# Moving rooms in SBUF so that loaded and moving operands stand at other distances modulo 512 bytes, and alternating halves in the gather

## The chip, the cores and the metric

The kernel runs on one core of a Trainium2 chip. The metric is device time in microseconds for one execution, the median of several. TensorE is called PE here, VectorE DVE, ScalarE ACT, GpSimd POOL and SyncE SP, as the profile calls them.

## The reference

There are 64 batches of 256 rows with 512 columns, and an adjacency matrix of 256 by 256 of zeros and ones. Two layers follow each other, each on a normalized and rectified copy of its input and added to that input:

```python
h = jnp.maximum(_layernorm(x, axis=-1), 0.0)
q = jnp.einsum('bnd,ed->bne', h, Wq);  k = jnp.einsum('bnd,ed->bne', h, Wk);  v = jnp.einsum('bnd,ed->bne', h, Wv)
rel = adjacency.T[None, :, :] * jnp.einsum('bnd,bmd->bnm', q, k)
rel = rel / jnp.linalg.norm(rel, axis=2, keepdims=True)
x = x + jnp.einsum('bnm,bmd->bnd', rel, v)

h = jnp.maximum(_layernorm(x, axis=-1), 0.0)
y = jnp.einsum('nm,bmd->bnd', adj, h)
x = x + jnp.einsum('bnd,do->bno', y, weight) + bias
```

## The kernel before

The batches are worked in 32 pairs, so the rows of a pair make 512. Wq and Wk are multiplied into one matrix m beforehand, so that the scores are h m h'.

A product of two float32 matrices is made of three rounds. Each operand is split into three parts: u, the value scaled and rounded to the format that PE reads in one pass; l, the rest; and s, a scaled combination of the two. The names end in those letters: h_u, h_l and hs (the third part of h, in two rooms hs0 and hs1), m_u, m_l, m_s, wv_u and so on, gy_u, gy_l, gy_s, rel_u, rel_l and rel_s. Rounds u by u and l by l are written into a PSUM bank. ACT then rescales the bank in place (L324), and round s by s is added. ACT and DVE split what comes out of a bank again (L225, L226, L228 for a part that later moves; L234, L235, L236 for one that is later loaded).

In each matrix product one operand is loaded into PE (128 by 128, the rows "PEld" of the profile) and the other moves through it. The load for the next product runs beside the current one. For one pair i the stages, each in units of one PSUM bank, are these:

- g: loaded m, moving h, 512 columns. Four units. The result goes into gy.
- v: loaded h, moving wv, 512 columns. Four units, of which two come before the scores and two after the gather. The result goes into v_low and late (one list of twelve rows; the first four are v_low).
- scores: loaded gy, moving h, 256 columns, two batches into one bank each.
- gather of pair i-1: loaded late or v_low (the second layer's h, in two parts), moving adjt (the turned adjacency), 256 columns, four units, each of two halves of a bank. The result goes into gy again.
- mix of pair i-1: loaded gy, moving w, 512 columns, four units.
- attend: loaded rel, moving late or v_low, 512 columns, four units. Then the second layer's normalization and rectification (L266, into rel_s_raw) and its split (L500, L501) follow, and POOL adds the bias (L504).

A pair has 168 products of 512 columns and 80 of 256. Between the scores and attend, the masked scores (L399) are squared and summed by ACT (L403), moved by sixteen small DMAs of SP (L439), and turned by DVE (L445). The next pair's h is likewise placed by DMAs (L280), turned by DVE (L288) into the rooms of hs, and split (L303, L305, L295). The order on each engine is fixed by a planner: each operation has an estimated cost and a due time worked out back from PE's ideal sequence, and the list is written out once and kept. The rescale of one unit is followed by the next unit's first two rounds and only then by the unit's own third round.

SBUF rooms are taken one after the other in the order in which the code first names their tags. Each takes its bytes per partition, rounded up to 32. The first room, fresh, starts at byte 16,512, which is 128 modulo 512. Rooms of whole multiples of 512 bytes keep the residue. The small rooms (ones, low_max, low_any, the statistics, the norms) move it to 32 for all that comes after them.

Of the kernel before, what the change touches and what calls it, by code (L numbers as in the profile page):

```python
# [10 lines left out]
F32R = mybir.dt.float32r  # L11
# [102 lines left out]
def kernel(  # L114
# [12 lines left out]
    P = 128  # L127
    B, N, D = x.shape
    DC = D // P
    NC = N // P  # L130
    NB = 2
    TC = NB * NC
    T = NB * N
# [9 lines left out]
    def room(name, *shape, dtype=F32, tag=None):  # L143
        return pool.tile([P, *shape], dtype, name=name, tag=tag or name)

    def parts_room(name, *shape, tag=None):
        return [room(f"{name}_{k}", *shape, dtype=F32R, tag=f"{tag or name}_{k}") for k in "uls"]
# [1 line left out]
    bank = [ps_m.tile([P, 512], F32, name=f"bank{n}") for n in range(8)]  # L149
    fresh = room("fresh", TC, D)  # L150
    ring = [room(f"x_ring{n}", TC, D) for n in range(2)]
    m_p, wv_p, w_p = (parts_room(w, DC, D) for w in ("m", "wv", "w"))
    h = [room(f"h_{k}", DC, T, dtype=F32R) for k in "ul"]
    ht, h_s = [None, None], [None, None]

    def hp(k, d):
        return h[k][:, d] if k < 2 else h_s[d // 2][:, d % 2]
    wq_sb, wk_sb = room("wq_sb", DC, D, tag="gy_u"), room("wk_sb", DC, D, tag="gy_l")
    adj_low = room("adj_low", 2, D, tag="rel_u")
    v_low = room("v_low", 4, D, dtype=F32R)  # L160
    blocks = room("blocks", TC, DC, P)
# [10 lines left out]
    def changing(tag, kind, *shape, dtype=F32):  # L172

        if rooms.get(tag, (None, None))[0] != kind:
            rooms[tag] = kind, room(f"{tag}_{kind}", *shape, dtype=dtype, tag=tag)
        return rooms[tag][1]

    def late(r):

        return v_low[:, r] if r < 4 else changing("late", "parts", 8, D, dtype=F32R)[:, r - 4]  # L180
# [16 lines left out]
        for j in range(2)  # L197
    ]
    norms = [room(f"rn{n}", NB, NC) for n in range(2)]

    V, A, G, SP = nc.vector, nc.scalar, nc.gpsimd, nc.sync
    count = {"bank": 0}
# [11 lines left out]
    def mm(out, left, right, first):  # L214
        nc.tensor.matmul(out, left, right, start=first, stop=True, skip_group_check=True)  # L215
# [15 lines left out]
    def split_left_ps(plan, ps, key, parts, names, at):  # L231
        u, l, s = (p(at) for p in parts)
        ku, kl, ks = names
        plan.add("ACT", 0.49, lambda: A.activation(u, ps, AF.Copy, scale=NEAR), [key], ku)  # L234
        plan.add("DVE", 0.6, lambda: V.tensor_sub(l, ps, f(u)), [key, *ku], kl)  # L235
        plan.add("DVE", 0.6, lambda: V.scalar_tensor_tensor(  # L236
            s, f(l), CROSS + 1.0, ps, op0=ALU.mult, op1=ALU.subtract), [key, *kl], ks)
# [3 lines left out]
    def load(plan, i, src=None, name="fresh"):  # L241

        dst = fresh if name == "fresh" else ring[i % 2]
        plan.add("SP", 0.65, lambda: SP.dma_start(out=dst, in_=xs[i]), [], keys(name, TC), lands=5.5)
# [70 lines left out]
    def unit(plan, first, second, drain):  # L315

        ps, key = next_bank()
        for cost, fn, reads in first(ps):
            plan.add("PE", cost, fn, reads, [key])
        finish(plan)  # L320
        if second is None:
            drain(ps, key)
            return
        plan.add("ACT", 0.49, lambda: A.activation(ps, ps, AF.Copy, scale=ONE), [], [key])  # L324

        def rest():
            for cost, fn, reads in second(ps):
                plan.add("PE", cost, fn, reads, [key])
            drain(ps, key)
        waiting.append(rest)  # L330
# [176 lines left out]
    def gather(plan, i, exact):  # L507
        right = adjt[0]
        for b in range(NB):
            for d0 in range(0, DC, 2):  # L510
                def first(ps, b=b, d0=d0):
                    def go():
                        for d in range(2):
                            for m in range(NC):
                                c = b * NC + m
                                lefts = [late(3 + 2 * c + k) for k in range(2)] if exact else [
                                    changing("late", "h2", 8, D)[:, c]]
                                for n, left in enumerate(lefts):
                                    mm(ps[:, ts(d, N)], left[:, ts(d0 + d, P)], right[:, m, :],
                                       d == 0 and m == 0 and n == 0)  # L520
                    needs = ["adjt", *(
                        ("late", r) for m in range(NC) for c in [b * NC + m]
                        for r in ((3 + 2 * c, 4 + 2 * c) if exact else (4 + c,)))]
                    yield 8 * HALF if exact else 8 * 0.216, go, needs

                def drain(ps, key, b=b, d0=d0):
                    split_left_ps(
                        plan, ps.rearrange("p (d n) -> p d n", d=2), key,
                        [lambda at, q=q: q[:, d0 : d0 + 2, ts(b, N)] for q in gy],
                        [[(f"gy_{k}", d0, b), (f"gy_{k}", d0 + 1, b)] for k in "uls"], None)  # L530
                unit(plan, first, None, drain)
# [52 lines left out]
    def before_pairs():  # L584
        A.activation(norms[1][:, 0, 0:1], ones, AF.Sqrt)
        for _ in range(8):
            mm(bank[7][:, :P], warm, warm, True)
        V.tensor_single_scalar(low, adj_low[:, 0].bitcast(I32), 0xFFF, op=ALU.bitwise_and)
        V.tensor_reduce(low_max, low, axis=mybir.AxisListType.X, op=ALU.max)
        m_products(0)  # L590
        mm(bank[7][0:1, 0:1], low_max, ones, True)
        V.tensor_copy(low_any, bank[7][0:1, 0:1])
        for m in range(NC):
            for n in range(NC):
                nc.tensor.transpose(bank[6][:, ts(m * NC + n, P)], adj_sb[:, n, ts(m, P)], ident)
        for e in range(1, DC - 1):
            m_products(e)
        plan = Plan()
        h_rows(plan, 0, ring[0], "x0")
        plan.run()  # L600

    with tc.manual_schedule(engines=in_order):
        before_pairs()
    gy = parts_room("gy", DC, T)
    rel_p = [room(f"rel_{k}", NB, NC, NC, P, dtype=F32R) for k in "ul"]
    adjt = []
    inexact = nc.values_load(low_any[0:1, 0:1], min_val=0, max_val=P * 0xFFF)
# [21 lines left out]
    def last_m(plan):  # L629
        for i in range(DC):  # L630
            plan.add("PE", 0.86, lambda i=i: m_products(DC - 1, (i,)), [], [("bank", i)])
            split_right_ps(plan, bank[i], ("bank", i), [lambda at, q=q: q[:, at, :] for q in m_p],
                           [[("m_u", i)], [("m_l", i)], [("m_s", i)]], i)
# [32 lines left out]
    def pairs(exact):  # L666
        count["bank"] = 4
        waiting.clear()
        rooms.clear()
        plan = Plan()  # L670
        adjt[:] = [room("adjt_r", NC, N, dtype=F32R, tag="adjt") if exact else room("adjt", NC, N)]
        plan.add("ACT", 0.49, lambda: A.copy(adjt[0].rearrange("p m n -> p (m n)"), bank[6]), [("bank", 6)], ["adjt"])
        first_turn(plan)
        last_m(plan)
        count["bank"] = 4
        turn_wv(plan)
        h_rows(plan, 1)
        h_place(plan, 25.0)
        load(plan, 2)
        first_g(plan)  # L680
        v_stage(plan, 0, exact, (0, 1))
        scores(plan, 0)
        v_stage(plan, 0, exact, (2, 3))
        turn_scores(plan, 0, by_pe=True)
        finish(plan)
        h_turn(plan)
        h_parts(plan)
        split_w(plan)
        attend(plan, 0, exact)
        for i in range(1, NP):  # L690
            last = i + 1 == NP
            load(plan, i, name=f"x{i % 2}")
            if not last:
                h_rows(plan, i + 1)
                h_place(plan)
            if i + 2 < NP:
                load(plan, i + 2)
            g_stage(plan, i)
            v_stage(plan, i, exact, (0,))
            v_stage(plan, i, exact, (1,), hold=True)  # L700
            scores(plan, i)
            gather(plan, i - 1, exact)
            while held:
                held.pop(0)()
            if last or i == 1:
                turn_scores(plan, i, by_pe=True)
            v_stage(plan, i, exact, (2, 3))
            if not last:
                if i > 1:
                    turn_scores(plan, i)  # L710
                waiting.append(lambda: (h_turn(plan), h_parts(plan)))
                mix(plan, i - 1)
            attend(plan, i, exact)
            if last:
                mix(plan, i - 1)
                gather(plan, i, exact)
            store(plan, i - 1)
        mix(plan, NP - 1)
        finish(plan)
        with tc.manual_schedule(engines=in_order):  # L720
            plan.run()
# [33 lines left out]
```

## Time and profile before

| | us |
|---|---|
| median of 3 runs | 1604.11 (1603.72 to 1604.55) |
| the profiled execution's own time | 1605.16 |
| its span | 1603.3 |
| rescale L324 on ACT, 572 times | 332.4 busy, 581 ns each |
| bias addition L504 on POOL, 128 times | 191.7 busy, 1517 ns each |
| gather, adjt by late_parts, 896 products | 124.6 busy, 282 ns each |
| mix, w_s by gy_s, 512 products | 139.9 busy, 395 ns each |
| gy_l, L228 on DVE, 128 times | 113.9 busy, 892 ns each |

The times of products are longer than the distance between two of them, because a product's record reaches from its issue to its end, and the next one is issued before that. The share of busy time of PE therefore says little about its pace; the starts of successive rows do. The page's row of the granted clock is at full speed in each of its 40 slices. A DMA of 64 KB that places h lands 2.1 us after its issue, and one of 32 KB that places the scores 1.9 us.

### The profile page before, as it was taken

How to read it: one execution, taken by the hardware profiler on the slowest of the kernel's cores; microseconds unless marked ns; L12 is line 12 of the kernel's file. 1: busy time of each engine (PE TensorE's matmuls, PEld its weight loads, DVE VectorE, ACT ScalarE, POOL GpSimd, SP SyncE). 2: the span in 40 equal slices, each digit the busy share in tenths (PEclk: the TensorE clock that was granted, in tenths of full speed). 3: DMA queues.
4: the chain of work that ended last, by engine and by line, in shares of the span. 5: the costliest groups of instructions: out<-in, count | busy, mean ns of one | idle time of the engine just before them, and what ended most of it. 6: DMA issues, size and time to landing. Idle time of an engine off the chain costs nothing.

```text
span 1603.3 us, 22542 instructions
## 1 busy us (share of the span) xinstructions
PE 1586.2 (99%) x8046; PEld 1332.9 (83%) x8046; DVE 1426.4 (89%) x2419; ACT 955.0 (60%) x1812; POOL 216.5 (14%) x167
## 2 busy tenths in 40 slices
PE   8999999999999999999999999999999999999998
PEld 5788888888888888888888888888888888888886
DVE  6998899998998988998988999889989889989886
ACT  5556566566556565665565665656565656656553
POOL 0011111011111011110111110111100111101111
PEclk9999999999999999999999999999999999999999
DMA  5431444324444224443234442244432344432311
GB/s 192 111 79 41 115 109 118 67 73 111 111 113 101 74 78 117 108 116 70 75 106 114 110 119 63 76 113 110 115 95 72 84 117 108 118 68 77 80 53 55
DMA packets 433130, 153.64 MB, mean 96 GB/s; under 512 B 389872, under 2 KB 390128, under 8 KB 433008
## 3 DMA queue, kind: packets, MB, share of 16 engines
q1 hardware_dynamic: 422784, 116.46, 30.8%
q0 software_dynamic: 8432, 32.51, 5.5%
q10 hardware_dynamic: 1792, 3.15, 0.5%
q8 instruction: 65, 1.06, 0.3%
q14 instruction: 57, 0.47, 0.1%
HBM read 70.78 MB, written 33.55 MB: 65 GB/s over the span
## 4 chain that ended last, share of the span: by engine, by line
PE 71%; DVE 16%; SPq 4%; ACT 3%; DMA 3%; issue 1%; DVEq 0%; ACTq 0%
PE bank L215 71%; SPq L439 3%; DVE st L252 3%; DVE late_parts L501 2%; DVE gy_l L228 2%; DVE gy_s L226 2%; DVE x_ring L480 1%; SPq L280 1%; DVE hs L295 1%; DVE mv L253 1%; DMA x_ring<-in_L_gnn_weight_dram 1%; DMA fresh<-in_x_dram 1%; DMA h_rel<-h_rel 1%; ACT rel_s_raw L266 1%; ACT h_rel L266 1%
## 5 line engine op out<-in xcount | busy, mean ns | idle before, releaser
L324 ACT ACTIVATE bank<-bank 128x512 f32<-128x512 f32 x572 | 332.4, 581 | 414.7 <-PE bank L215 414.0
L504 POOL TENSOR_TENSOR x_ring<-x_ring,bias_bc 128x512 f32<-128x512 f32 x128 | 191.7, 1517 | 387.4 <-ACT rel_s_raw L266 387.4
L551 POOL DMA_DIRECT2D out_dram<-x_ring x31 | 24.0, 774 | 982.1 <-DVE x_ring L542 982.1
L215 PE MATMUL bank<-w_s,gy_s 128*128 128x512 f32 x512 | 139.9, 395 | 0.2 <-ACT bank L324 0.2
L215 PE MATMUL bank<-wv_s,hs 128*128 128x512 f32 x512 | 139.9, 395 | 0.0
L215 PE MATMUL bank<-w_u,gy_u 128*128 128x512 f32 x512 | 139.6, 394 | 0.0
L215 PE MATMUL bank<-wv_u,h_u 128*128 128x512 f32 x512 | 139.4, 394 | 0.0
L215 PE MATMUL bank<-h_u,m_u 128*128 128x512 f32 x512 | 138.9, 393 | 0.3 <-DVE m_s L226 0.3
L215 PE MATMUL bank<-hs,m_s 128*128 128x512 f32 x512 | 139.1, 394 | 0.0
L215 PE MATMUL bank<-w_l,gy_l 128*128 128x512 f32 x512 | 138.6, 392 | 0.0
L215 PE MATMUL bank<-wv_l,h_l 128*128 128x512 f32 x512 | 138.0, 391 | 0.0
L215 PE MATMUL bank<-h_l,m_l 128*128 128x512 f32 x512 | 137.5, 391 | 0.1
L226 DVE SCALAR_TENSOR_TENSOR gy_s<-gy_u,bank 128x512 fp32r<-128x512 f32 x128 | 86.3, 676 | 44.1 <-ACT gy_u L225 41.9
L215 PE MATMUL bank<-adjt_r,late_parts 128*128 128x256 f32 x896 | 124.6, 282 | 0.0
L228 DVE SCALAR_TENSOR_TENSOR gy_l<-gy_s,gy_u 128x512 fp32r<-128x512 f32 x128 | 113.9, 892 | 4.3
L215 PEld LDWEIGHTS bank<-adjt_r,late_parts 128*128 128x128 f32 x896 | 115.5, 190 | 0.1
L215 PEld LDWEIGHTS bank<-w_s,gy_s 128*128 128x128 f32 x512 | 95.9, 188 | 23.5 <-ACT bank L324 0.9
L215 PEld LDWEIGHTS bank<-h_u,m_u 128*128 128x128 f32 x512 | 96.0, 188 | 23.0 <-ACT wv_u L225 0.5
L215 PEld LDWEIGHTS bank<-w_u,gy_u 128*128 128x128 f32 x512 | 96.0, 188 | 22.7
L215 PEld LDWEIGHTS bank<-h_l,m_l 128*128 128x128 f32 x512 | 96.1, 188 | 21.9 <-DVE h_l L305 0.5
L215 PEld LDWEIGHTS bank<-w_l,gy_l 128*128 128x128 f32 x512 | 96.1, 188 | 21.8
L215 PEld LDWEIGHTS bank<-hs,m_s 128*128 128x128 f32 x512 | 96.3, 188 | 21.4
(109 smaller groups left out, 3241.7 us busy)
## 6 DMA issues: line engine op xcount, KB each, us to landing
fresh<-in_x_dram SPq DMA_DIRECT2D x31, 1024.0 KB, 6.0
blocks<-h_rel SPq DMA_DIRECT2D x496, 64.0 KB, 2.1
x_ring<-in_x_dram SPq DMA_DIRECT2D x31, 1024.0 KB, 7.9
out_dram<-x_ring POOLq DMA_DIRECT2D x31, 1024.0 KB, 5.2
h_rel<-h_rel SPq DMA_DIRECT2D x464, 32.0 KB, 1.9
blocks<-in_L_gnn_Wv_dram ACTq DMA_DIRECT2D x1, 1024.0 KB, 11.2
x_ring<-in_L_gnn_weight_dram SPq DMA_DIRECT2D x1, 1024.0 KB, 12.6
out_dram<-x_ring SPq DMA_DIRECT2D x4, 256.0 KB, 2.3
```

The source lines that it names most:

```text
L215: nc.tensor.matmul(out, left, right, start=first, stop=True, skip_group_check=True)
L226: plan.add("DVE", 0.63, lambda: V.scalar_tensor_tensor(s(), f(u()), ONE, ps, op0=ALU.mult, op1=ALU.subtract), [*key, *ku], ks)
L228: plan.add("DVE", 0.6, lambda: V.scalar_tensor_tensor(l(), f(s()), -CROSS, f(u()), op0=ALU.mult, op1=ALU.add), [*ku, *ks], kl)
L252: V.bn_stats(st[:, c, :], src[:, c, :])
L253: V.bn_aggr(mv[:, c, :], st[:, c, :])
L266: A.activation(dst, src[:, c, :], AF.Relu, bias=nb[:, c : c + 1], scale=rs[:, c : c + 1])
L280: plan.add("SP", 0.65, lambda j=j, k=k: SP.dma_start(out=blocks[ts(j, S), :, :, ts(k, S)], in_=hv[ts(k, S), :, :, ts(j, S)]), keys("h_rel" ...
L324: plan.add("ACT", 0.49, lambda: A.activation(ps, ps, AF.Copy, scale=ONE), [], [key])
L439: plan.add("SP", 0.65, lambda j=j, k=k: SP.dma_start(out=pv[ts(j, S), :, ts(k, S)], in_=rv[ts(k, S), :, ts(j, S)]), [("h_rel", 0), ("h_rel ...
L501: plan.add("DVE", 0.6, lambda c=c, u=u, l=l: V.tensor_sub(late(l), raw()[:, c % 2], f(late(u))), [*k, ("late", u)], [("late", l)])
L504: plan.add("POOL", 1.4, lambda c=c: G.tensor_tensor(ring[slot][:, c, :], ring[slot][:, c, :], bias_bc, ALU.add), [], [(f"x{slot}", c)])
L551: plan.add("POOL", 0.8, lambda: G.dma_start(out=outs[i], in_=ring[slot]), keys(f"x{slot}", TC), [], lands=6.0)
```

## The change

It does three things. First, it changes the order in which rooms are first named, and adds two rooms that nothing writes or reads: "behind" of 160 bytes per partition, and "level" of 448. The three parts of w, wq_sb and wk_sb (whose rooms gy_u and gy_l take over later) and gy_s now come behind the small rooms. Second, the turned adjacency gets a room larger by 512 bytes, and lies 448 bytes into it. Third, the gather's innermost loop now runs over the two halves of the bank; before, each half was finished ahead of the other.

```diff
-    m_p, wv_p, w_p = (parts_room(w, DC, D) for w in ("m", "wv", "w"))
+    m_p, wv_p = (parts_room(w, DC, D) for w in ("m", "wv"))
-    wq_sb, wk_sb = room("wq_sb", DC, D, tag="gy_u"), room("wk_sb", DC, D, tag="gy_l")
...
     norms = [room(f"rn{n}", NB, NC) for n in range(2)]
+    room("behind", 40)
+    w_p = parts_room("w", DC, D)
+    wq_sb, wk_sb = room("wq_sb", DC, D, tag="gy_u"), room("wk_sb", DC, D, tag="gy_l")
+    gy_s = room("gy_s", DC, T, dtype=F32R)
+    room("level", 112)
...
-                        for d in range(2):
-                            for m in range(NC):
-                                c = b * NC + m
-                                lefts = [late(3 + 2 * c + k) for k in range(2)] if exact else [
-                                    changing("late", "h2", 8, D)[:, c]]
-                                for n, left in enumerate(lefts):
+                        for m in range(NC):
+                            c = b * NC + m
+                            lefts = [late(3 + 2 * c + k) for k in range(2)] if exact else [
+                                changing("late", "h2", 8, D)[:, c]]
+                            for n, left in enumerate(lefts):
+                                for d in range(2):
                                     mm(ps[:, ts(d, N)], left[:, ts(d0 + d, P)], right[:, m, :],
                                        d == 0 and m == 0 and n == 0)
...
-    gy = parts_room("gy", DC, T)
+    gy = [*(room(f"gy_{k}", DC, T, dtype=F32R) for k in "ul"), gy_s]
...
-        adjt[:] = [room("adjt_r", NC, N, dtype=F32R, tag="adjt") if exact else room("adjt", NC, N)]
+        turned_adj = room("adjt_r", NC * N + P, dtype=F32R, tag="adjt") if exact else room("adjt", NC * N + P)
+        adjt[:] = [turned_adj[:, P - 16 : P - 16 + NC * N].rearrange("p (c n) -> p c n", c=NC)]
```

The residues modulo 512 bytes, worked out from the sizes of the rooms (slices of an operand move by multiples of 512, so a room has one residue):

| room | before | after |
|---|---|---|
| m, wv (all parts), h_u, h_l, rel_u, v_low | 128 | 128 |
| w (all parts), gy_u, gy_l | 128 | 192 |
| gy_s | 32 | 192 |
| rel_l, hs, late, rel_s | 32 | 128 |
| adjt | 32 | 64 |

The text calls "distance" the residue of the moving operand less that of the loaded one. For 512-column products it was 0 in rounds u and l of g, v and mix, and 96 or -96 in round s; in attend it was 0 or 96 or -96, by the pair of rooms. For 256-column ones it was 0 in the scores and, in the gather, 0 for late and -96 for v_low. Afterwards it is 0 for every 512-column product and -64 for every 256-column one.

## The prediction, made before the changed kernel was built or run

> **What bounds the kernel now.** I read the page first. By its shares one engine is the bound:
>
> ```profile
> PE 1586.2 (99%) x8046; PEld 1332.9 (83%) x8046; DVE 1426.4 (89%) x2419; ACT 955.0 (60%) x1812; POOL 216.5 (14%) x167
> ```
>
> The clock row is full speed throughout, so pace is a matter of the products. Products overlap, so I take the pace from the timeline of PE: the difference of the starts of two rows, over the count.
>
> ```profile
> 27.22 3.89 PE L215 MATMUL bank<-h_u,m_u 128*128 128x512 f32 x16 [0.31 <-DVE m_s L226]
> 30.95 3.79 PE L215 MATMUL bank<-h_l,m_l 128*128 128x512 f32 x16
> 34.57 0.63 PE L215 MATMUL bank<-hs,m_s 128*128 128x512 f32 x2
> ...
> 755.04 1.09 PE L215 MATMUL bank<-hs,m_s 128*128 128x512 f32 x4
> 755.97 1.09 PE L215 MATMUL bank<-h_u,m_u 128*128 128x512 f32 x4
> 756.89 1.07 PE L215 MATMUL bank<-h_l,m_l 128*128 128x512 f32 x4
> 757.80 1.09 PE L215 MATMUL bank<-hs,m_s 128*128 128x512 f32 x4
> ```
>
> Sixteen h_l by m_l products in a row run at (34.57-30.95)/16 = 226 ns. Both operands lie at residue 128 (the table of residues is in the section on the change): distance 0. In the steady state, hs by m_s, at distance 96, takes 0.93/4 = 232 ns; h_u by m_u, at distance 0 but just behind such a group, takes 0.92/4 = 230; h_l by m_l behind that takes 227.5. So I read: distance 0 settles at 226.7, distance 96 costs about 6 ns a product, and some eight products behind a change of distance still pay part of it. Now the 256-column ones, in the gather, where v_low lies at distance 96 from adjt and late_parts at 0:
>
> ```profile
> 726.28 0.28 PE L215 MATMUL bank<-adjt_r,v_low 128*128 128x256 f32 x1
> 726.39 0.52 PE L215 MATMUL bank<-adjt_r,late_parts 128*128 128x256 f32 x3
> 726.75 0.27 PE L215 MATMUL bank<-adjt_r,v_low 128*128 128x256 f32 x1
> 726.87 2.43 PE L215 MATMUL bank<-adjt_r,late_parts 128*128 128x256 f32 x19
> 729.14 1.09 PE L215 MATMUL bank<-wv_u,h_u 128*128 128x512 f32 x4
> ```
>
> Nineteen at distance 0 take 2.27/19 = 119.5 ns. The four from 726.28 take 117.5, and the second v_low product 110 to 120. Distance helps here, where it hurts the 512-column ones.
>
> Is PE's pace what sets the end, though? The waits (who waited for whom: us in all, times, longest) and the timeline of DVE:
>
> ```profile
> DVE ht L288 <- PE bank L215: 8.1, 29, 0.3
> ...
> PEld bank L215 <- DVE gy_l L228: 7.2, 30, 0.7
> ```
>
> ```profile
> 736.27 1.30 DVE L288 STREAM_TRANSPOSE ht<-blocks 128x512 f32<-128x512 f32 x2 [0.28 <-PE bank L215]
> ...
> 758.39 0.16 DVE L262 SCALAR_TENSOR_TENSOR nb<-mv,rs 128x4 f32<-128x4 f32 x1
> ```
>
> Once in each pair of batches DVE waits for PE (the transposes of h may not overwrite the third part before PE's last use of it), and once PE waits for DVE (the last gy_l). Between 736.27 and nb, which ends at 758.55, the timeline shows DVE without an idle bracket: 22 us back to back. ScalarE's first rectification (L266) starts at 758.65; its other condition, the rescale L324 ahead of it, ends at 758.58, so the two paths meet within 0.03 us. From there the chain of waits goes on:
>
> ```profile
> 758.65 0.82 ACT rel_s_raw L266
> ...
> 761.40 2.31 DVE late_parts L501 x2
> ...
> 772.98 0.18 DVE rs L256
> ```
>
> It holds no PE work up to the root L258, behind which the rescale L324 stands in ScalarE's queue, for which PE's hs by gy_s waits at 773.9 (as at 725.23 a pair earlier). So a pair of 48.7 us is 11.1 us of PE, from 725.23 to 736.3, and then 37.6 us of DVE and ScalarE. Only what PE gains in the first piece comes out at the end; a gain in the other piece becomes a longer wait on gy_l or on L324.
>
> **What the Trainium skill says.** No page bears on the distance of two operands modulo 512 bytes; the trace alone prices it. "TensorE: Matmul & The Clock Gate", section Back-to-back issue gap, gives N/2.4 + 2.5 ns for a product alone: 215.8 and 109.2 ns; the trace shows 226 to 232 and 119.5, so 10 to 16 ns go elsewhere. The section LDWEIGHTS there gives columns/1.2, 107 ns for 128: as long as a 256-column product streams, half a 512-column one; so in the former load and stream share the whole time, and the two kinds need not want the same distance. "SBUF — State Buffer", section Who interferes with whom, says that PE never waits on anyone and that a DVE instruction with two SBUF inputs is held up by a GpSimd one that reads SBUF. The second agrees: gy_l takes 693 ns in the median and up to 1546, beside POOL's bias additions. That lengthens the DVE piece, and the change leaves it alone.
>
> **The change part by part.**
>
> The rooms: from their sizes, all 512-column pairs come to distance 0 (hs with m_s and wv_s, w_s with gy_s, late with rel_u, v_low with rel_l and rel_s are the ones that were not) and all 256-column pairs to -64. No instruction is added; the reserved rooms are written by none, and the queues of SP and POOL keep their order.
>
> 512 columns, in the 11.1 us piece: 32 products (two v blocks, the third parts, the first half of a mix unit). Their time now: starts from 729.14 to 736.54, 7.40 us, 231.3 ns each. Ends for the price after: 226.7 (settled) and 231.3 (no gain). The first eight follow 256-column work and mix lies at 192 where v lies at 128, so some unsettling stays: I take 229. Gain 32 x 2.3 = 74 ns.
>
> 256 columns, same piece: 8 scores products and 24 of the gather. The trace shows 96, not 64. Ends: 110 ns, the shortest gap shown, and 128: 8 ns over now, somewhat above what distance costs a 512-column product, since load and stream overlap all along. I take 114, between the 110 and the 117.5 of the mixed groups. Gain 32 x (119.5-114) = 176 ns.
>
> Halves alternating in the gather: same products, same costs, another order within one unit. The scores already alternate between halves and run at the same 120 ns, so zero by itself; up to 2 ns either way on 24 products if it matters at the new pace, inside the ends above.
>
> The tie at L266: the other condition (PE's path) ends sooner, at best 0.03 us a pair.
>
> Sum a pair: 0.074 + 0.176 + 0.03 = 0.28 us, 29 pairs of this form: 8.1 us. The other 48 256-column and 136 512-column products of a pair gain some 0.6 us and give it back as waits: cover enough that they cost nothing even if slower by a few ns. Can the 0.28 pass? DVE's idle time just ahead of the transposes is 0.28 us, and what stands before it (late_parts, waiting 0.56 us for ScalarE and PE) moves up too. The score transposes need their DMAs; between the last landing and DVE's start I find about 1 us in most pairs and 0.1 to 0.3 in some eight: these may give back a little.
>
> At the end (last pair: no next batch to place, DVE idle for 1 to 2.8 us at a time) PE is the bound: some 144 512-column products at 2.3 and 64 256-column ones at 5.5 ns: 0.33 + 0.35 = 0.7 us. The start is bound by loads and the first splits: nothing.
>
> In all 8.8 us off. The profiled span was 1603.3 us and its execution 1605.16; the median of the runs 1604.11, so I set the sum against that: 1595.3 us.
>
> **The rivals.**
>
> PE's gain passes whole, if the 37.6 us are not as rigid as I read them (PE and DVE meet there within 0.03 us, so DVE's chain might move with PE's). 5,376 x 2.3 + 2,560 x 5.5 ns = 12.4 + 14.1 = 26.5 us: 1577.6. For it: PE at 99%; against: the two waits in every pair.
>
> Only the 512-column products gain, 64 being no better than 0 for the short ones: 29 x (0.074 + 0.03) + 0.3 = 3.3 us: 1600.8. For it: scores at distance 0 behind an offset group run at 117 to 119 as well, so the 117.5 may be the disturbance and not the distance.
>
> The distance of 64 hurts the short products: at 128 ns each, the 11.1 us piece takes 32 x 8.5 = 272 ns more, 74 less for the long ones: 0.2 x 29 = 5.7 us, and a little at the end: 1610. It decides above 121.8 ns (119.5 + 74/32). For it: distance 96 hurts the long ones; against: the v_low products.
>
> The layout does not come out as computed (an unwritten room gets no space): then weights, gy and late stay at 32 and nothing changes: 1604.
>
> **How the numbers follow.** Mine 0.58, full gain 0.14, little 0.15, slower 0.10, layout 0.03. With the price of a short product from 110 to 118, mine spans 1590 to 1600. The range reaches down half way into the full gain, and up over "little" to the edge of the slower case: 1580 to 1604. 0.2% is 3.2 us, what a measurement of this kernel tells from no change. Faster: mine, full gain and a bit under half of "little": 0.79. Same: the rest of "little", the layout case, some of the slower one: 0.12. Slower: 0.09.
>
> **What would show it.** Right: s groups at 227 to 229; scores and gather under 118; PE's waits on gy_l and L324 longer by some 0.4 us a pair; the DVE piece still 37.6 us; the pair 48.4. Wrong: a period shorter by 0.8 us with those waits as before (full gain), short products at 120 (little) or above 122 (slower).

## The result, and the profile after

| | median us | runs |
|---|---|---|
| before | 1604.16 (1603.72 to 1607.27) | 5 |
| after | 1595.87 (1594.7 to 1597.74) | 5 |

The ratio is 0.9946, with a 95% interval of 0.9931 to 0.996: 8.3 us less. The forecast was 1595.3. The profiled execution has a span of 1594.1 us. All line numbers of the kernel after are seven higher: L215 is now L222, L228 is L235, L324 is L331.

The page's share line, and its chain that ended last:

```profile
PE 1566.8 (98%) x8046; PEld 1327.2 (83%) x8046; DVE 1423.1 (89%) x2419; ACT 953.1 (60%) x1812; POOL 216.2 (14%) x167
...
DVE 43%; PE 42%; ACT 5%; SPq 4%; DMA 3%; issue 2%; DVEq 0%; ACTq 0%
```

The shares hardly differ from before, and the chain does. This was the chain before, and ACT before at the rectification L266, where PE's path (through the rescale L324) meets that of DVE (through nb, which ends at 758.55 us):

```profile
PE 71%; DVE 16%; SPq 4%; ACT 3%; DMA 3%; issue 1%; DVEq 0%; ACTq 0%
```

```profile
758.00 0.58 ACT L324 ACTIVATE bank<-bank 128x512 f32<-128x512 f32 x1 [1.00 <-PE bank L215]
758.65 0.82 ACT L266 ACTIVATE rel_s_raw<-x_ring,nb,rs 128x512 f32<-128x512 f32 x1
```

Before, the two paths ended within 0.04 us of each other in 24 of 30 pairs, and the chain could follow either. Now DVE's ends later in every pair, by 0.1 us or more.

The timeline of PE after, at the gather and then where hs by m_s stood out before:

```profile
720.84 1.21 PE L222 MATMUL bank<-hs,gy_s 128*128 128x256 f32 x8
721.89 0.40 PE L222 MATMUL bank<-adjt_r,v_low 128*128 128x256 f32 x2
722.13 2.66 PE L222 MATMUL bank<-adjt_r,late_parts 128*128 128x256 f32 x22
724.63 1.08 PE L222 MATMUL bank<-wv_u,h_u 128*128 128x512 f32 x4
...
731.96 1.09 PE L222 MATMUL bank<-w_u,gy_u 128*128 128x512 f32 x4
...
752.91 1.07 PE L222 MATMUL bank<-hs,m_s 128*128 128x512 f32 x4
753.82 1.07 PE L222 MATMUL bank<-h_u,m_u 128*128 128x512 f32 x4
754.72 1.07 PE L222 MATMUL bank<-h_l,m_l 128*128 128x512 f32 x4
755.63 1.07 PE L222 MATMUL bank<-hs,m_s 128*128 128x512 f32 x4
```

Read the starts. The gather's 22 take (724.63-722.13)/22 = 113.6 ns in this pair, one of the faster ones, and the 32 long products behind them (731.96-724.63)/32 = 229.1 ns. All three rounds of h by m now go at (755.63-752.91)/12 = 226.7 ns, where one of them took 232 and unsettled its neighbours. Over the whole trace, taking all gaps of starts without a stall (under 300 ns for 512 columns, under 170 for 256), the means are:

| gap of starts, ns | before | after | all distances 0 (a run below) |
|---|---|---|---|
| 512 columns, 5,376 products | 231.2 | 227.7 | 227.0 |
| 256 columns, 2,560 products | 119.2 | 116.7 | 119.6 |

So PE alone has gained 5376 x 3.5 + 2560 x 2.5 ns = 25 us, and 8.3 arrive. Most of the rest stands in the waits (us in all, times, longest):

```profile
PEld bank L222 <- DVE gy_l L235: 18.5, 30, 1.1
...
PE bank L222 <- DVE gy_l L235: 12.5, 30, 0.9
...
PEld bank L222 <- ACT bank L331: 7.8, 23, 1.6
...
DVE ht L295 <- PE bank L222: 7.9, 29, 0.3
```

The first and the fourth were 7.2 and 8.1 us before, as the prediction shows; these are the other two before:

```profile
PE bank L215 <- DVE gy_l L228: 1.6, 5, 0.5
...
PEld bank L215 <- ACT bank L324: 3.9, 7, 1.6
```

(The two rows on gy_l are the same wait seen by the load and by the product, so they are not added.) The median stall of a pair for gy_l has grown from 0.23 to 0.56 us, that for the rescale from 0.09 to 0.23.

The table follows one pair through the two pieces of the prediction: medians over 25 pairs in the middle of the trace, in us.

| | before | after |
|---|---|---|
| first piece, PE's product after the rescale to DVE's transposes | 11.04 | 10.95 |
| of it: 8 of the scores | 1.047 | 1.033 |
| of it: 24 of the gather | 2.862 | 2.828 |
| of it: 512-column products until the transposes | 7.137 | 7.093 |
| second piece, from the transposes to PE's next such product | 37.66 | 37.41 |
| of it: transposes to the end of rs | 20.49 | 20.46 |
| of it: end of rs to the start of gy_s | 0.095 | -0.092 |
| of it: start of gy_s to the end of nb | 1.70 | 1.69 |
| of it: end of nb to the rectification | 0.095 | 0.096 |
| of it: rectification to PE's product | 15.27 | 15.25 |
| pair | 48.70 | 48.36 |

The second piece was to be rigid, and it is shorter by 0.25 us. Three quarters of that are in one row, between rs and gy_s. This is the timeline of DVE before at that spot, and then that of ACT before, in one pair:

```profile
707.89 0.17 DVE L256 TENSOR_SCALAR rs<-mv 128x4 f32<-128x4 f32 x1
708.16 0.69 DVE L226 SCALAR_TENSOR_TENSOR gy_s<-gy_u,bank 128x512 fp32r<-128x512 f32 x1
```

```profile
707.53 0.60 ACT L225 ACTIVATE gy_u<-bank 128x512 fp32r<-128x512 f32 x1 [0.41 <-PE bank L215]
```

And after, DVE and then ACT:

```profile
752.51 0.17 DVE L263 TENSOR_SCALAR rs<-mv 128x4 f32<-128x4 f32 x1
752.59 0.68 DVE L233 SCALAR_TENSOR_TENSOR gy_s<-gy_u,bank 128x512 fp32r<-128x512 f32 x1
753.30 0.69 DVE L235 SCALAR_TENSOR_TENSOR gy_l<-gy_s,gy_u 128x512 fp32r<-128x512 f32 x1
753.91 0.17 DVE L268 RECIPROCAL rs<-rs 128x4 f32<-128x4 f32 x1
754.11 0.16 DVE L269 SCALAR_TENSOR_TENSOR nb<-mv,rs 128x4 f32<-128x4 f32 x1
```

```profile
753.11 0.58 ACT L331 ACTIVATE bank<-bank 128x512 f32<-128x512 f32 x1 [0.19 <-PE bank L222]
754.37 0.81 ACT L273 ACTIVATE rel_s_raw<-x_ring,nb,rs 128x512 f32<-128x512 f32 x1 [0.68 <-DVE nb L269]
```

Before, gy_s starts at 708.16, 0.10 us after rs has ended (708.06) and 0.03 after the end of ACT's gy_u (708.13); and the bracket of gy_u shows that it waits for PE's bank. So a thread from PE ran through the middle of the DVE piece. The gap is too short for the timeline to put a bracket on it. Afterwards the record of gy_s begins before that of rs has ended, and gy_u has been ready for 0.16 us in the median. The kernel before confirms the reading by itself: in five of its pairs gy_u was ready 0.14 us or more ahead, and there, too, gy_s begins 0.09 us before rs has ended.

### The profile page after: what moved, and what is told of

Its sections match the earlier page's. It is cut to its first block, busy times and chain, and to the rows that moved or that the text cites. A ratio compares the mean times of both kernels' runs of the same rounds, so it can differ in the third digit from the quotient of the medians.

```text
span 1594.1 us, 22542 instructions
## 1 busy us (share of the span) xinstructions
PE 1566.8 (98%) x8046; PEld 1327.2 (83%) x8046; DVE 1423.1 (89%) x2419; ACT 953.1 (60%) x1812; POOL 216.2 (14%) x167
## 4 chain that ended last, share of the span: by engine, by line
DVE 43%; PE 42%; ACT 5%; SPq 4%; DMA 3%; issue 2%; DVEq 0%; ACTq 0%
PE bank L222 42%; DVE st L259 7%; DVE gy_l L235 7%; DVE x_ring L487 5%; DVE late_parts L508 5%; DVE gy_s L233 5%; DVE hs L302 4%; SPq L446 3%; DVE x_ring L549 2%; DVE mv L260 2%; ACT rel_s_raw L273 2%; SPq L287 1%; ACT gy_u L232 1%; DVE h_l L312 1%; DMA fresh<-in_x_dram 1%
## 5 line engine op out<-in xcount | busy, mean ns | idle before, releaser
L331 ACT ACTIVATE bank<-bank 128x512 f32<-128x512 f32 x572 | 332.3, 581 | 395.7 <-PE bank L222 393.3
L511 POOL TENSOR_TENSOR x_ring<-x_ring,bias_bc 128x512 f32<-128x512 f32 x128 | 191.4, 1515 | 382.3 <-ACT rel_s_raw L273 382.3
L222 PE MATMUL bank<-wv_s,hs 128*128 128x512 f32 x512 | 138.5, 392 | 0.4 <-ACT bank L331 0.4
L222 PE MATMUL bank<-w_u,gy_u 128*128 128x512 f32 x512 | 138.0, 391 | 0.0
L222 PE MATMUL bank<-wv_u,h_u 128*128 128x512 f32 x512 | 137.7, 391 | 0.0
L222 PE MATMUL bank<-w_s,gy_s 128*128 128x512 f32 x512 | 137.4, 390 | 0.4 <-ACT bank L331 0.4
L222 PE MATMUL bank<-w_l,gy_l 128*128 128x512 f32 x512 | 137.4, 390 | 0.0
L222 PE MATMUL bank<-wv_l,h_l 128*128 128x512 f32 x512 | 137.3, 390 | 0.0
L222 PE MATMUL bank<-h_u,m_u 128*128 128x512 f32 x512 | 136.5, 389 | 0.3 <-DVE m_s L233 0.3
L222 PE MATMUL bank<-h_l,m_l 128*128 128x512 f32 x512 | 136.6, 389 | 0.1
L222 PE MATMUL bank<-hs,m_s 128*128 128x512 f32 x512 | 136.3, 389 | 0.0
L235 DVE SCALAR_TENSOR_TENSOR gy_l<-gy_s,gy_u 128x512 fp32r<-128x512 f32 x128 | 113.7, 890 | 4.3
L273 ACT ACTIVATE rel_s_raw<-x_ring,nb,rs 128x512 f32<-128x512 f32 x128 | 100.6, 810 | 24.9 <-DVE late_parts L508 15.6
L222 PE MATMUL bank<-adjt_r,late_parts 128*128 128x256 f32 x896 | 115.1, 280 | 0.0
L222 PEld LDWEIGHTS bank<-w_s,gy_s 128*128 128x128 f32 x512 | 95.9, 188 | 21.1 <-ACT bank L331 1.1
L222 PEld LDWEIGHTS bank<-w_u,gy_u 128*128 128x128 f32 x512 | 96.0, 188 | 20.8
L222 PEld LDWEIGHTS bank<-w_l,gy_l 128*128 128x128 f32 x512 | 96.1, 188 | 20.7
L222 PEld LDWEIGHTS bank<-wv_l,h_l 128*128 128x128 f32 x512 | 96.1, 188 | 20.5
L222 PEld LDWEIGHTS bank<-h_u,m_u 128*128 128x128 f32 x512 | 96.0, 188 | 20.5 <-ACT wv_u L232 0.5
L222 PEld LDWEIGHTS bank<-h_l,m_l 128*128 128x128 f32 x512 | 96.0, 188 | 20.4 <-DVE h_l L312 0.5
```

The lines of the kernel that those rows point to most:

```text
L235: plan.add("DVE", 0.6, lambda: V.scalar_tensor_tensor(l(), f(s()), -CROSS, f(u()), op0=ALU.mult, op1=ALU.add), [*ku, *ks], kl)
L273: A.activation(dst, src[:, c, :], AF.Relu, bias=nb[:, c : c + 1], scale=rs[:, c : c + 1])
L511: plan.add("POOL", 1.4, lambda c=c: G.tensor_tensor(ring[slot][:, c, :], ring[slot][:, c, :], bias_bc, ALU.add), [], [(f"x{slot}", c)])
```

## The experiments

The theory to test: the rooms quicken PE's products by the distance of their two operands; a part of this comes through, and the rest is taken by a chain of DVE and ACT that is as long as a pair. The rivals: the order of the gather does it; the distance of -64 is worth nothing beside 0; the chain isn't the bound, and something else gives the gain back.

**The order of the gather alone**, on the kernel before (the same exchange of loops as in the change's diff, nothing else):

> The gather's order alone, rooms as before. If only the distances matter: gather products at distance 0 stay at 119 to 120 ns, time 1604 us, within 2. If alternating halves is what made the short products faster: gather at 117 ns, and 24 of them in the piece of a pair that counts give 29 x 24 x 2.5 ns = 1.7 us, 1602 us.

Measured: 1604.9 us against 1604.78 before, ratio 1.0002 (0.9994 to 1.0011). The gather in its timeline of PE:

```profile
725.83 2.80 PE L215 MATMUL bank<-adjt_r,late_parts 128*128 128x256 f32 x22
728.46 1.09 PE L215 MATMUL bank<-wv_u,h_u 128*128 128x512 f32 x4
```

2.63/22 = 119.5 ns, the pace of before. **The rooms alone**, the kernel after with the old order of the gather:

```diff
-                        for m in range(NC):
+                        for d in range(2):
+                            for m in range(NC):
...
-                                for d in range(2):
```

> The rooms alone, gather's halves one after the other as before. If the distances are all of it: the time of the whole change, 1596 us within 1.5; gather at 116 to 117 ns. If the alternation carries part of it: gather at 119 ns or above, 1598 us.

1594.8 us, ratio 0.9941 (0.9928 to 0.9955); the pieces of a pair are those of the kernel after (10.95 and 37.41 us). All of the gain is the rooms', none the order's.

**All distances 0**: w, gy and adjt at residue 128, like the rest.

```diff
-    room("behind", 40)
+    room("behind", 24)
...
-    room("level", 112)
...
-        adjt[:] = [turned_adj[:, P - 16 : P - 16 + NC * N].rearrange("p (c n) -> p c n", c=NC)]
+        adjt[:] = [turned_adj[:, 0 : 0 + NC * N].rearrange("p (c n) -> p c n", c=NC)]
```

> The change with distance 0 for the 256-column products too (w, gy and adjt at residue 128). Short products back at 120 ns, long ones at 227. If only PE's work in the first 11 us of a pair counts: 32 long products gain 32 x 4 ns = 0.13 us, 29 pairs 3.8 us, 0.5 us at the end: 1600 us. If all of PE's gain passes: 5,376 x 4 ns = 21 us: 1583 us. If the distance of 64 was worth nothing: 1596 us as the whole change.

1596.15 us, ratio 0.995 (0.9937 to 0.9964): not to be told from the whole change, where I had looked for a loss. The timeline of PE, at the gather:

```profile
722.47 2.80 PE L221 MATMUL bank<-adjt_r,late_parts 128*128 128x256 f32 x22
725.11 1.09 PE L221 MATMUL bank<-wv_u,h_u 128*128 128x512 f32 x4
```

2.64/22 = 120 ns: the short products have lost what -64 gave them. In the first piece this is 2.880 us for the gather, 0.052 more than after. But the 512-column products behind it take 7.027 us, 0.066 less, since no room at 192 stands among those at 128. The two cancel, and the piece is 10.94 us. So in this kernel the distance of 0 for the long products is worth the whole change, and -64 for the short ones nothing more.

**Is DVE's chain the bound?** If it is, a DVE that is shorter elsewhere must let PE's gain through. In the chain after, between the rectification and PE's next product, two operations of DVE take far more than their usual time (0.68 us each):

```profile
754.37 0.81 ACT rel_s_raw L273
755.18 0.49 ACT gy_u L232
...
757.12 2.30 DVE late_parts L508 x2
...
760.05 1.53 DVE gy_l L235
...
763.80 0.70 DVE gy_l L235
764.50 0.04 issue
764.55 4.50 PE bank L222 x32
```

The two of L508 take 2.30 us together, and gy_l takes 1.53 once and 0.70 the next time. POOL adds the bias just then. "SBUF — State Buffer" in the Trainium skill, section Who interferes with whom, has DVE and GpSimd share a pair of SBUF ports under an exclusive lock. So the adds of the pair were held until the masked scores of the next pair had been written, which comes later in the pair (those of the last pair follow its gather at once):

```diff
+    def add_bias(plan, i, after_scores=True):
+        slot = i % 2
+        if after_scores:
+            plan.add("POOL", 0.1, lambda: G.tensor_copy(low_max, rel[:, 1, 0, 0:1]), [("h_rel", 1)], ["low"])
         for c in range(TC):
             plan.add("POOL", 1.4, lambda c=c: G.tensor_tensor(
-                ring[slot][:, c, :], ring[slot][:, c, :], bias_bc, ALU.add), [], [(f"x{slot}", c)])
+                ring[slot][:, c, :], ring[slot][:, c, :], bias_bc, ALU.add), ["low"], [(f"x{slot}", c)])
...
             scores(plan, i)
+            add_bias(plan, i - 1)
...
                 gather(plan, i, exact)
+                add_bias(plan, i, False)
```

> The change, and POOL's bias additions held back until DVE has masked the scores, so that they no longer lie beside DVE's instructions with two SBUF inputs in the long chain (1.0 us at late_parts L501 and 0.85 at gy_l in each pair). If that chain sets the pair: PE becomes the bound, a pair takes 168 x 227.7 + 80 x 116.6 ns + 0.2 = 47.8 us in place of 48.4, and 29 pairs bring 17 us: 1579 us, with PE's wait on gy_l gone. If PE was the bound all along and the waits only the form it took: 1596 us, no change.

1595.51 us, ratio 0.9943 (0.9929 to 0.9956). This tells nothing, because the hold did not hold. Its timeline of POOL, and that of DVE beside it:

```profile
705.56 3.00 POOL L516 TENSOR_TENSOR x_ring<-x_ring,bias_bc 128x512 f32<-128x512 f32 x2 [7.57 <-ACT rel_s_raw L273]
```

```profile
707.32 1.78 DVE L508 TENSOR_TENSOR late_parts<-rel_s_raw,v_low 128x512 fp32r<-128x512 f32 x1
```

The adds still follow the rectification and still stand beside L508. At that point of the list the planner had not yet been given the operation that writes the pair's masked scores, so the wait was put on an older one, long done. Called behind the gather, whose first unit gives the planner that operation, the wait names the right writer:

```diff
             scores(plan, i)
-            add_bias(plan, i - 1)
             gather(plan, i - 1, exact)
+            add_bias(plan, i - 1)
```

> As e4, whose additions were not held back (the wait that it gave POOL was met long before); here POOL reads one masked score of the current pair ahead of the additions. If DVE's long chain sets the pair: it loses up to 1.85 us, PE becomes the bound at 168 x 227.7 + 80 x 116.6 ns + 0.2 = 47.8 us a pair in place of 48.4, 1579 us, and PE's wait on gy_l falls under 0.3 us a pair. If PE was the bound all along: 1596 us.

1573.2 us (1571.77 to 1575.55), ratio 0.9805 (0.9792 to 0.9818). POOL's timeline, the source view of L508 (shortest, median and longest in ns), the waits, and the page's share line and chain, all of this kernel:

```profile
712.74 0.18 POOL L514 COPY low_max<-h_rel 128x1 f32<-128x1 f32 x1 [23.48 <-DVE h_rel L406]
712.88 5.05 POOL L516 TENSOR_TENSOR x_ring<-x_ring,bias_bc 128x512 f32<-128x512 f32 x4
```

```profile
L508 DVE TENSOR_TENSOR late_parts<-rel_s_raw,v_low x32: 659/685/692, 81.6 to 1545.5; 128x512 fp32r<-128x512 f32 x32
```

```profile
PEld bank L222 <- DVE gy_l L235: 1.6, 4, 0.8
PE bank L222 <- DVE gy_l L235: 0.6, 1, 0.6
```

```profile
PE 1556.2 (99%) x8046; PEld 1325.0 (84%) x8046; DVE 1366.7 (87%) x2419; ACT 953.5 (61%) x1812; POOL 192.9 (12%) x198
...
PE 85%; DVE 6%; DMA 3%; SPq 3%; ACT 2%; issue 1%; DVEq 0%; ACTq 0%
```

In the kernel after, the same L508 row is

```profile
L508 DVE TENSOR_TENSOR late_parts<-rel_s_raw,v_low x32: 678/1780/1793, 82.8 to 1568.2; 128x512 fp32r<-128x512 f32 x32
```

1780 ns becomes 685, the wait on gy_l goes from 18.5 to 1.6 us, and PE is 85% of the chain. PE, DVE and ACT run the same operations in the same order in both kernels' traces; only POOL's work has moved. So the chain of DVE was the bound, and POOL's adds made it long. This version beats both kernels.

**The same hold on the kernel before**:

> The same hold on the additions in the kernel before. If DVE's chain and PE's pace bound it alike there: a pair falls from 48.7 us to PE's 168 x 231.2 + 80 x 119.3 ns + 0.2 = 48.6 us, so 1600 us, and the rooms are worth some 22 us next to e5, most of PE's whole gain. If the additions themselves are what costs: as much off as in e5, 1587 us.

1593.11 us, ratio 0.9929 (0.9915 to 0.9943). Its chain:

```profile
PE 92%; DVE 4%; DMA 2%; ACT 1%; SPq 0%; issue 0%; DVEq 0%
```

Neither expectation (1600 or 1587 us) was met: the hold takes 12.2 us off the kernel before. A pair takes 48.37 us in the mean, which is the sum of PE's gaps without any wait (168 x 231.2 + 80 x 119.1 ns); the 0.2 us added to that sum in the expectation aren't there. The pair of the kernel before takes 48.74, so DVE's chain held that kernel back as well, by 0.37 us a pair, although its paths looked like a tie at L266. With DVE out of the way the rooms are worth 1593.11-1573.2 = 19.9 us instead of 8.3; so the gain that the kernel after gave back was there. The mean gaps of the two traces (231.2 and 119.1 against 227.7 and 116.6 ns) would give 25. Most of the other 5 us are waits that are left in the kernel after with the hold: its pair takes 47.74 us in the mean and the sum of its gaps is 47.58, so 0.16 us a pair, 4.6 us in 29. **All distances 0, with the hold:**

> The hold, with all distances 0 as in e3. PE's sum a pair: 168 x 227.0 + 80 x 119.6 ns + 0.2 = 47.9 us, so within 2 us of e5, 1580 us, if the distance of 64 only moves nanoseconds from the long products to the short ones. If 64 is worth what its short products show (3 ns on 80): 7 us over e5, 1586 us.

1576.99 us, ratio 0.9824 (0.981 to 0.9837), 3.8 us more than with -64, between the 2 and the 7 us expected. From the gaps (227.1 and 119.7 against 227.7 and 116.6 ns): 2560 x 3.1 - 5376 x 0.6 ns = 4.7 us. So -64 is worth something once PE is the bound, and only then.

**Which distance suits the short products?** +64 in the kernel after (behind 8, level 16, adjt at 16), and then -32, -128 and -256 in the kernel with the hold, in which PE is the bound. Each changes the same three numbers, as here for -32:

```diff
-    room("behind", 40)
+    room("behind", 32)
...
-    room("level", 112)
+    room("level", 120)
...
-        adjt[:] = [turned_adj[:, P - 16 : P - 16 + NC * N].rearrange("p (c n) -> p c n", c=NC)]
+        adjt[:] = [turned_adj[:, 120 : 120 + NC * N].rearrange("p (c n) -> p c n", c=NC)]
```

> The change with +64 in place of -64 for the 256-column products. If only the size of the distance counts: 116 to 117 ns and 1596 us. If it counts who runs ahead: short products at another pace, 119 ns or above as at 0, and 1596 to 1599 us.

> e5 with distance -32 for the 256-column products. PE is the bound there, so 1 ns on a short product is 2.5 us at the end. If the distance matters by its size, half of 64 gives some pace between 119.6 (0) and 116.5 (-64): 118 ns, 1575 us. If any distance but 0 does: 116.5 ns, 1573 us.

> e5 with distance -128. If a larger distance brings more: 114 ns or less and 1567 us. If any distance but 0 is alike: 1573 us. If 64 is where the gain lies, and the loss of long products at 96 comes back for short ones: over 119 ns, 1579 us or more.

> e5 with distance 256, half the period. If a larger distance brings more: 113 ns or less, 1565 us. If any distance but 0 is alike: 1573 us. If only a small one helps: 119 ns or above, 1579 us.

| distance of the 256-column products | their gap, ns | time, us | ratio |
|---|---|---|---|
| +64 (kernel after) | 117.9 | 1596.23 | 0.9944 (0.9929 to 0.9959) |
| -64 (kernel after) | 116.7 | 1595.87 | 0.9946 (0.9931 to 0.996) |
| 0 (with the hold) | 119.7 | 1576.99 | 0.9824 (0.981 to 0.9837) |
| -32 (with the hold) | 118.4 | 1575.53 | 0.9826 (0.981 to 0.9843) |
| -64 (with the hold) | 116.6 | 1573.2 | 0.9805 (0.9792 to 0.9818) |
| -128 (with the hold) | 119.4 | 1575.69 | 0.9822 (0.9806 to 0.9839) |
| -256 (with the hold) | 119.7 | 1575.29 | 0.9821 (0.9805 to 0.9838) |

The ratios of the last five overlap at their edges, and -32, -128 and -256 were measured beside other runs of the kernel before (1604.17 us in the median, against 1605.33 for 0 and -64 with the hold), so the times alone order them poorly; the gaps do it better. By them -32 and +64 lie between 0 and -64, which neither expectation for +64 had, and -128 and -256 bring next to nothing, though their times stayed under the 1579 us that were expected for that case.

The means at +64 and -64 hide something. Taking the last 16 products of late_parts in each of the 32 gathers of a trace, a gather runs at 113.3 ns or at 117.8, at +64 as at -64, and at nothing between. The faster pace is taken by 3 gathers at +64, by 6 at -64 in the kernel after, and by 23 at -64 with the hold. So the runs don't show that the sign matters: for the gather the means differ by how often the faster pace is taken. In the timeline of PE at -256 the gather is back at the pace of distance 0:

```profile
713.94 2.80 PE L222 MATMUL bank<-adjt_r,late_parts 128*128 128x256 f32 x22
716.59 1.09 PE L222 MATMUL bank<-wv_u,h_u 128*128 128x512 f32 x4
```

2.65/22 = 120.5 ns. And its long products, in which rooms 256 apart in residue alternate, have the smallest mean next to all zero: 227.06 ns.

## Why the prediction was right, by its own steps

- **512 columns at distance 0, 74 ns a pair.** The mechanism is as read: 232 became 226.7. The price of 229 for the 32 of the first piece was 229.1 in the pair shown, against 231.3. In the median pair the time from the first of them to the transposes fell by 44 ns, so the term was too large by 30.
- **256 columns at -64, 176 ns a pair.** The mis-sized term. The 114 ns are reached in 6 of 32 gathers (113.6 in the one shown); the mean over the trace is 116.7, and in the first piece the median pair has 2.828/24 = 117.8. Of the 176 ns, 34 came from the gather and 14 from the scores.
- **The order of the gather, zero.** Shown by the two runs that part it from the rooms.
- **The tie at L266, 0.03 us.** Nothing: the rectification starts 95 ns behind nb before and 96 after, and it does so, too, in the pairs before in which the rescale ended well ahead of nb. So DVE's nb released it already.
- **A rigid second piece.** Here the reading was incomplete. "Back to back" was read from missing idle brackets, and gaps of 0.1 us carry none. In that gap gy_s waited for ACT's gy_u, and this for PE; 0.19 us a pair came from there.
- **The sum.** Expected 0.28 us a pair; in the medians it is 0.09 + 0.25 = 0.34, in the means of the period 48.74-48.44 = 0.30, and with 29 pairs 8.7 us. The total agreed because one term that was too large and one that was missed are of about one size: 0.16 us less in the first piece, 0.22 more in the second. So the closeness of the forecast is luck in this part, and no precision.
- **The end, 0.7 us.** About right: from the first piece of the last pair with transposes to the end of the span it is 97.93 us before and 97.05 after, 0.9 less. With it the two profiled spans differ by 9.2 us; the medians of the runs differ by 8.3.
- **Load and stream share the whole time of a short product.** This was argued from 107 ns for a load, and no run here shows it: the trace's records of loads last 188 ns each, from issue to end.
- **What is given back, where.** Longer waits on gy_l and on L324 by 0.4 us a pair: measured 0.33 + 0.14. The cause, DVE's chain, was shown by shortening it.

Of the rivals, the full gain (26.5 us) is what PE's gaps did gain (25) and what mostly came through (19.9) once DVE was freed. "Little" had a true observation in it: beside a bound DVE, 0 does as well as -64. But its reason, that only the long products gain, fails: the short ones went from 119.2 to 116.7 ns. So the term on which the forecast leaned most, 176 of 280 ns, wasn't needed for the result, as the run with all distances 0 shows. That 64 hurts them, which needed more than 121.8 ns, falls with the same number, and the layout came out as computed.

## What to carry to other kernels

Read the gap between starts by the pair of operands, because two products of one shape can differ by some per cent through nothing but where their rooms lie; a reserved room is then a cheap edit. Before counting such a gain, find the wait in which it would end: here two thirds of it went into waits, most of them for one operation of DVE, and moving POOL's work away from DVE brought more than the change itself. In a chain that looks rigid, compare each start with the end of what it needs, and not only the brackets: behind a gap of 0.1 us lay more than half of this change's effect (0.19 of 0.34 us a pair).

## What the runs showed of the hardware

- The pace of products back to back depends on the addresses of the loaded and the moving operand relative to each other. With 512 columns 0 is better than 96 or -96 (226.7 ns settled, 232 for hs by m_s at -96); with 256 columns -64 has the lowest mean of the values tried (116.6 ns, against 119.7 at 0). The section of the SBUF page named above gives PE two independent read ports for the two operands. By these figures the two don't run without effect on each other; whether the ports are where they meet, no run here shows.
- The loaded operand that counts is at least in part that of the next product, whose load runs beside the current one. The runs with the hold share three changes of stage (v to mix, mix to attend, mix to v) at which a long product's own distance is 0 and only the next product's loaded operand lies elsewhere. The mean gap of these 150 products is 226.8 ns when the next one lies at 0 too and, either way, 234.3 at 32, 229.9 at 64, 232.5 at 128 and 227.0 at 256. In the kernel before, the 414 long products of own distance 0 whose next load was 96 away, either way, took 234.3 ns, and the 317 of own distance 96 or -96 whose next load was at 0 took 230.5. The distances in the section on the change are those of a product's own two operands. Inside a group of products that is the same thing, at its end it isn't.
- The residues were counted modulo 512 bytes, but 256 do: -256 gives the short products 119.7 ns, as 0 does, and costs the long ones nothing (227.0 above). For the long ones 128 is too short a period, as 232.5 ns there show; for the short ones, 119.4 at -128, it isn't excluded.
- The pace has a memory. Behind a change of residue or of the number of columns, long products take 225 to 236 ns, by turns, for five to sixteen products and then settle at 227; with all distances 0, too, the first five behind a gather do so. What chooses between 113.3 and 117.8 ns for a gather at a distance of 64 stays open.
- An operation of DVE with two inputs in SBUF took 1780 ns beside POOL's adds and 685 without them, more than double, and POOL's own mean fell from 1515 to 1304 ns with the adds elsewhere.
